# A post-norm attention and low-rank-expert layer: the FFN taken tile by tile, its narrow products joined to the wide ones, and the prior gathered first

## The chip, the cores and the metric

The kernel runs on one core of one Trainium2 chip. The metric is the device time of one execution in microseconds (us). A core has five engines that run side by side, each working through its own list of instructions in order: TensorE (PE: matrix products into PSUM banks), VectorE (DVE), ScalarE (ACT), GpSimd (POOL) and SyncE (SP, which only issues transfers here). An engine that reaches an instruction whose input is not ready stands still, and everything behind that instruction in its list stands with it. A PSUM bank that is to be written again must first have been read out.

## The reference

Two batches of 512 tokens, 512 features, all in 32-bit floats. The layer is two steps, each followed by a layer norm:

```
x = layernorm(x + attention(x))      # 32 query heads, 8 key/value heads of 128, causal, rotary
x = layernorm(x + ffn(x))

ffn(x):  y     = x @ W_base.T + b_base
         z_e   = x @ lora_A[e].T                     # 4 active experts of 16, rank 8
         alpha = softmax(log(prior + 1e-12) + router logits)     # over the 4 active ones
         y    += sum over e of alpha_e * 2 * (z_e @ lora_B[e].T)
```

The indices of the active experts are an input (`active`), so the rows of `lora_A`, `router_W`, `router_b`, `domain_prior` and `lora_B` have to be gathered at run time.

## The kernel before

The 1024 tokens are eight tiles of 128 (four per batch). Attention is 16 units (a key/value head of one batch) of four query tiles, so 64 parts; each part has four score blocks of 128 rows. The main loop is a software pipeline written out by hand: `slot(T)` issues one score block, and beside it pieces of work of other parts at fixed distances: projections for later units (L333, L346, and the query projection by Strassen products, L420), the softmax of the blocks before (maximum L487, exponential L494, reciprocal L498, normalise L502), the transposes of the probabilities (L510, L512), their way through DRAM (store, then `pT` load L528, both issued by SP), the product with the values (L535, `weigh`, into the one bank `pc` of the pool `ps_ctx`, copied out by ACT at L541), and the output projection (L420 for most parts, `wo_mm` L606 and `wo_out` L612 for the last eight). `put(slot, f)` hangs further work onto a slot. Nothing reorders this: the program is under a manual schedule, and every engine's list is the order in which the lines are written.

*The gathers.* POOL issues the loads of `active` early (L209 to L212: `act_e`, four of `act_er`, `act_p`). `gather_experts` runs in slot -8: eleven small integer operations on DVE turn the indices into row numbers, and POOL issues eight indirect gathers: A, router weights, router bias, prior, and four of B. In slots -4 to -2, `prior_weights` uses two of them: DVE adds a small number (L295), ACT takes the logarithm (L297), DVE adds the bias and spreads the row (L300, L304), and TensorE multiplies by the identity (`pl`, L307) so that all 128 partitions hold it. In slots 12 to 16 `lora_weights` transposes the gathered rows into `arT` (32 columns of A and 4 of the router) and `bmT` (B, with `b_base` as a 33rd row).

*The FFN.* `wbT` holds the transposed W_base. The class `Ffn` handles a group of tiles: `f0` is two pairs (batch 0), `fa` a pair, `fb` and `fc` one tile each (batch 1, whose last four parts are attended in the order 2, 3, 0, 1). For a tile x1T, the normed and transposed tokens, TensorE does:

- `route` (L665): four matmuls with the 36 columns of `arT`, giving `zl` (z and router logits), in a bank of its own;
- `base` (L712): four matmuls with the 512 columns of `wbT` into `py`;
- `low_rank` (L706): a transpose of `zs` (z times alpha), which DVE then copies (L707) to `zT`;
- `finish` (L716): one matmul of `zT` and `bmT` added into `py`; DVE adds x (L719) and takes the statistics for the second norm.

Between `route` and `low_rank` stand the softmax over the four experts (`logits` and `alphas`: DVE, ACT, DVE). The last tile `fc` does its W_base product in two halves (`half`, L727 to L729) whose banks DVE reads without an add. Each 32-bit matmul is two records in the trace.

A norm (`Norm`) is statistics on DVE, a square root on ACT (L631) and a reciprocal and a scaling on DVE (L635). Square root and exponential are different tables of ACT, so a change between them is an ACT_TABLE_LOAD. Stores of finished tiles are issued by SP, behind whatever stands before them in SP's list.

*Order.* With A = 245 as the slot in which the last Strassen output projection starts and E = 256 as the end of the score blocks: the first pair of `f0` does `route` at A+5, `base` at A+6 to A+9, the transposes at A+8, `finish` at A+10 and its stores at A+11. The second pair does `route` at A+13, its first tile's `base` at A+14 and A+15, and the rest in the tail, a list of calls behind the last slot. In that tail `base` of one tile stands between `route` and `low_rank` of another throughout:

```
    fa.low_rank()
    for c in range(KC):
        fa.base(1, c, *SC)
    fb.low_rank()
    fc.route(0)
```

Of the kernel before, what the change touches and what calls it, by code (L numbers as in the profile page):

```python
# [29 lines left out]
def postln_layer_kernel(  # L30
# [85 lines left out]
    bqkT = const.tile([P, H + G], F32, name="bqkT")  # L116
    arT = const.tile([P, KC, EAR + EA], F32, name="arT")
# [52 lines left out]
    nc.vector.memset(maskw, 0.0)  # L170
# [50 lines left out]
    def gather_experts():  # L221
# [25 lines left out]
        def gather(dst, src, idx):  # L247
            nc.gpsimd.indirect_dma_start(
                out=dst, out_offset=None, in_=src,
                in_offset=bass.IndirectOffsetOnAxis(ap=idx, axis=0),  # L250
            )

        gather(a_act, lora_A.rearrange("e r n -> (e r) n"), idx_a)
        gather(r_act, router_W, full_e)
        gather(rb_act, router_b.rearrange("(e o) -> e o", o=1), full_e)
        gather(pr_act, domain_prior.rearrange("(e o) -> e o", o=1), full_e)
        for a in range(EA):
            gather(b_act[:, a, :], lora_B.rearrange("e (p j) r -> (e p) (j r)", j=BJ), idx_b[:, a : a + 1])
# [379 lines left out]
    class Ffn:  # L638


        def __init__(self, name, tiles, pool, small_bank):
            self.name, self.pool, self.n = name, pool, len(tiles)
            self.small_bank = small_bank
            self.where = tiles
            self.tiles = [x_sb[:, t, :] for t in tiles]
            self.norm1 = Norm(pool, self.n, f"a{name}")
            self.norm2 = Norm(pool, self.n, f"f{name}")
            self.xT, self.py, self.y = {}, {}, {}

        def own(self, shape, name):  # L650
            return self.pool.tile(shape, F32, name=f"{name}_{self.name}")

        def centre(self, i):
            self.norm1.apply(i, self.tiles[i])

        def transpose(self, i, pool, tag):
            self.xT[i] = self.pool.tile([P, KC, P], F32, name=f"x1T_{self.where[i]}")
            transpose_token_tile(self.xT[i], self.tiles[i], pool, tag, nc.scalar.copy)

        def route(self, i):  # L660

            if i == 0:
                self.zl = self.small_bank[0].tile([P, self.n, EAR + EA], F32, tag=self.small_bank[1], name="zl")
            for c in range(KC):
                nc.tensor.matmul(  # L665
                    self.zl[:, i, :], lhsT=self.xT[i][:, c, :], rhs=arT[:, c, :],
                    start=(c == 0), stop=(c == KC - 1))

        def logits(self):
            n = self.n  # L670
            self.lg = self.own([P, n, EA], "lg")
            lp_all = lp_bc.unsqueeze(1).to_broadcast([P, n, EA])
            nc.vector.tensor_tensor(self.lg, self.zl[:, :, EAR:], lp_all, ALU.add)
            nmx = self.own([P, n], "nmx")
            nc.vector.tensor_reduce(nmx, self.lg, AX.X, ALU.max, negate=True)
            nc.vector.tensor_tensor(
                self.lg, self.lg, nmx.unsqueeze(2).to_broadcast([P, n, EA]), ALU.add)

        def alphas(self):

            n = self.n
            al = self.own([P, n, EA], "al")
            nc.scalar.activation(al, self.lg, AF.Exp)
            sm = self.own([P, n], "sm")
            nc.vector.tensor_reduce(sm, al, AX.X, ALU.add)
            nc.vector.reciprocal(sm, sm)
            nc.vector.tensor_scalar(sm, sm, SCALING, None, ALU.mult)
            nc.vector.tensor_tensor(al, al, sm.unsqueeze(2).to_broadcast([P, n, EA]), ALU.mult)
            self.zs = self.own([P, n, EA, RK], "zs")
            for i in range(n):  # L690
                nc.vector.tensor_tensor(
                    self.zs[:, i],
                    self.zl[:, i, :EAR].rearrange("p (a r) -> p a r", r=RK),
                    al[:, i, :].unsqueeze(2).to_broadcast([P, EA, RK]),
                    ALU.mult,
                )

        def ones(self):

            self.zT = self.own([EAR + 1, self.n, P], "zT")  # L700
            nc.gpsimd.memset(self.zT[EAR:, :, :], 1.0)

        def low_rank(self):
            tz = self.small_bank[0].tile([EAR, self.n, P], F32, tag=self.small_bank[1], name="tz")
            for i in range(self.n):
                nc.tensor.transpose(tz[:, i, :], self.zs[:, i].rearrange("p a r -> p (a r)"), ident)  # L706
            nc.vector.tensor_copy(self.zT[:EAR], tz)  # L707

        def base(self, i, c, pool, tag):
            if c == 0:  # L710
                self.py[i] = pool.tile([P, O], F32, tag=tag, name="py")
            nc.tensor.matmul(  # L712
                self.py[i], lhsT=self.xT[i][:, c, :], rhs=wbT[:, c, :], start=(c == 0), stop=False)

        def finish(self, i):
            nc.tensor.matmul(self.py[i], lhsT=self.zT[:, i, :], rhs=bmT, start=False, stop=True)  # L716
            t = self.where[i]
            self.y[i] = self.pool.tile([P, O], F32, name=f"y_{t}")
            nc.vector.tensor_tensor(self.y[i], self.py[i], self.tiles[i], ALU.add)  # L719
            self.norm2.stats(i, self.y[i])  # L720

        def half(self, i, n, pool, tag):

            cols = ts(n, O // 2)
            py = self.py[i, n] = pool.tile([P, O // 2], F32, tag=tag, name="ph")
            for c in range(KC):
                nc.tensor.matmul(py, lhsT=self.xT[i][:, c, :], rhs=wbT[:, c, cols], start=(c == 0), stop=False)  # L727
            nc.tensor.matmul(py, lhsT=ident, rhs=self.tiles[i][:, cols], start=False, stop=False)
            nc.tensor.matmul(py, lhsT=self.zT[:, i, :], rhs=bmT[:, cols], start=False, stop=True)  # L729

        def store(self, i):
            self.norm2.apply(i, self.y[i])
            nc.sync.dma_start(out=outf[ts(self.where[i], P), :], in_=self.y[i])

        def store_halves(self, i):
            t = self.where[i]
            y = self.pool.tile([P, O], F32, name=f"y_{t}")
            for n, queue in enumerate((nc.sync, nc.scalar)):
                cols = ts(n, O // 2)
                self.norm2.apply(i, y[:, cols], self.py[i, n])  # L740
                queue.dma_start(out=outf[ts(t, P), cols], in_=y[:, cols])
# [168 lines left out]
    for part in range(3):  # L910
        k_rope(0, part)

# [25 lines left out]
    wbT = ffn_pool.tile([P, KC, O], F32, name="wbT")  # L938
# [4 lines left out]
    K_BANK, WX, WY = (ps_k, "k"), (ps_wo, "wx"), (ps_wo, "wy")  # L943
    QX, QY, SC = (ps_q, "qx"), (ps_q, "qy"), (ps_sc, "sc")
    f0 = [Ffn(f"0{n}", [2 * n, 2 * n + 1], ffn_pool, K_BANK) for n in range(2)]
    fa = Ffn("1a", [TPB + i for i in order[:2]], ffn_pool, K_BANK)
    fb = Ffn("1b", [TPB + order[2]], ffn_pool, WX)
    fc = Ffn("1c", [TPB + order[3]], ffn_pool, WY)
    for f in (*f0, fa, fb, fc):
        f.ones()  # L950
    E = T_END
    A = LAST + LAG_WO
    for c in range(OC):
        put(T_PROJ + (0, 1, 4, 5)[c], lambda c=c: nc.sync.dma_start(out=wb_sb[:, c, :], in_=W_base[ts(c, P), :]))
        put(T_PROJ + (4, 5, 8, 9)[c], lambda c=c: transpose_token_tile(wbT[:, :, ts(c, P)], wb_sb[:, c, :], ps_k, "k", nc.scalar.copy))
    put(A + 1, lambda: [f.norm1.root(0, 2) for f in f0])
    for n, f in enumerate(f0):
        for k in range(2):
            put(A + (-7, -6, 0, 0)[2 * n + k], lambda f=f, k=k: f.norm1.stats(k, f.tiles[k]))
            put(A + 1 + n, lambda f=f, k=k: f.centre(k))  # L960
            put(A + 3 + n, lambda f=f, k=k: f.transpose(k, *(QX, QY)[k]))

    for n, f in enumerate(f0):
        at = A + 5 + n * 8
        for k in range(2):
            put(at, lambda f=f, k=k: f.route(k))
        put(at, f.logits)
        put(at + 1, f.alphas)
        for k in range(2 - n):
            for c in range(KC):  # L970
                put(at + 1 + 2 * k + c // 2, lambda f=f, k=k, c=c: f.base(k, c, *(QX, QY)[k]))
        put(at + 3, f.low_rank)
    for k in range(2):
# [11 lines left out]
    for k in range(2):  # L985
        fa.centre(k)
# [6 lines left out]
    for c in range(KC):  # L993
        fz.base(1, c, *QY)
# [100 lines left out]
```

## Time and profile before

| | us |
|---|---|
| three runs | 845.39, 845.54, 847.07 (median 845.54) |
| the profiled execution | 845.97 |
| its span, first to last instruction | 844.2 |
| TensorE busy in it | 830.7 |
| VectorE busy | 595.3 |
| ScalarE busy | 348.2 |
| GpSimd busy | 276.6 |
| mean granted TensorE clock | 0.996 |

The profile page names an engine, a line of the kernel (L716), an operation and its tiles as output<-inputs, with buffer numbers left out. "x8" is the number of records. In the chain of work that ended last, each instruction is followed back to what released it, and the shares of the span are given by engine. A line of waits reads: the waiting engine, its tile and line, what released it, then microseconds in all, how often, and the longest. A line of the table by windows gives the stretch, its length, then for PE, PEld (TensorE's loading of weights, which overlaps its matmuls), DVE, ACT and POOL in turn the microseconds busy with the count of instructions in brackets, and last the granted TensorE clock (1.00 is full speed), the busy share of the transfers, and GB/s. A timeline line is the start, the duration, the engine, and in square brackets how long the engine had been idle and what released it.

### The profile page before, as it was taken

Reading aid. Unit: us, or ns where it says so; the run is one execution under the profiler, and the core shown is the slowest. Engines: PE = TensorE matmul, PEld = TensorE weight load, DVE = VectorE, ACT = ScalarE, POOL = GpSimd, SP = SyncE. Lnnn points to the kernel's source line nnn. Section 1 sums busy time; section 2 is a strip of 40 time slices with the busy share of each in tenths; the row PEclk is TensorE's granted clock in tenths of the full one; section 3 lists DMA queues with packets and bytes.
Section 4 is the critical chain, followed back from the end, with each engine's and each line's share of the span. In section 5 each row is a group of like instructions: output and inputs, shape, how many; then the busy total and the mean of one; then the engine's idle time right before and its main releaser. Section 6 shows DMA issues by size and latency. Waiting matters only on the chain.

```text
span 844.2 us, 10656 instructions
## 1 busy us (share of the span) xinstructions
PE 830.7 (98%) x3179; PEld 578.1 (68%) x3179; DVE 595.3 (71%) x1955; ACT 348.2 (41%) x988; POOL 276.6 (33%) x307
## 2 busy tenths in 40 slices
PE   8989999999999999999999999999999999999997
PEld 5557677777777777777777777777777776645453
DVE  3458977778767876687767876687767868953545
ACT  1125454544435343434435443434435344662321
POOL 5375333422342334222342334334333523300000
PEclk9999999999999999999999999999999999999999
DMA  9016536445553546354553547275544536574302
GB/s 288 34 28 193 142 108 175 138 125 175 133 151 103 175 121 191 83 151 148 142 145 101 175 128 195 72 201 148 148 127 125 175 92 195 166 244 114 87 1 75
DMA packets 84971, 116.47 MB, mean 138 GB/s; under 512 B 6581, under 2 KB 64797, under 8 KB 82866
## 3 DMA queue, kind: packets, MB, share of 16 engines
q1 hardware_dynamic: 84258, 115.50, 48.0%
q0 software_dynamic: 448, 0.14, 0.3%
q8 instruction: 25, 0.41, 0.2%
q14 instruction: 32, 0.26, 0.1%
q10 hardware_dynamic: 208, 0.15, 0.1%
HBM read 71.73 MB, written 44.04 MB: 137 GB/s over the span
## 4 chain that ended last, share of the span: by engine, by line
PE 92%; DVE 4%; DMA 1%; POOL 1%; ACT 1%; issue 1%; SPq 0%; DVEq 0%; POOLq 0%
PE pc L535 16%; PE sc L479 13%; PE qx L420 11%; PE wx L420 11%; PE pp L346 9%; PE qy L420 8%; PE wy L420 8%; PE pv L333 7%; PE py L712 3%; PE po L606 3%; PE tp L265 1%; PE py L716 1%; PE zl L665 1%; DMA x_sb<-_attn_hidden_states_dram 1%; PE ph L727 0%
## 5 line engine op out<-in xcount | busy, mean ns | idle before, releaser
L494 ACT ACTIVATE p<-sc,nmax 128x288 f32<-128x288 f32 (+15 forms) x256 | 124.2, 485 | 266.0 <-DVE nmax L487 209.3
L487 DVE CUSTOM_DVE_ANT_0 sc<-sc,maskw 128x288 f32<-128x288 f32 (+15 forms) x256 | 114.2, 446 | 153.6 <-PE sc L479 150.9
L535 PE MATMUL pc<-pT,v 128*128 128x512 f32 x320 | 165.5, 600 | 0.0
L479 PE MATMUL sc<-kT,qT 128*128 128x160 f32 (+15 forms) x512 | 161.9, 398 | 1.3 <-ACT p L494 1.2
L502 ACT ACTIVATE p<-p,den 128x288 f32<-128x288 f32 (+15 forms) x256 | 133.5, 522 | 1.2 <-DVE den L498 1.0
L367 POOL TENSOR_TENSOR qT<-q,t 128x512 f32<-128x512 f32 x56 | 71.0, 1267 | 189.1 <-DVE q L366 189.1
L479 PEld LDWEIGHTS sc<-kT,qT 128*128 128x128 f32 x512 | 96.8, 190 | 31.0 <-issue 14.6
L407 POOL TENSOR_TENSOR cs<-ctxT 128x256 f32<-128x256 f32 x28 | 26.8, 956 | 195.6 <-PE wy L420 109.2
L541 ACT COPY ctxT<-pc 128x512 f32<-128x512 f32 x64 | 37.5, 586 | 119.3 <-PE pc L535 119.2
L510 DVE STREAM_TRANSPOSE zt<-p 128x128 f32<-128x128 f32 (+2 forms) x192 | 81.6, 425 | 0.0
L535 PEld LDWEIGHTS pc<-pT,v 128*128 128x128 f32 x320 | 56.9, 190 | 20.0 <-issue 6.4
L346 PE MATMUL pp<-xT,wk 128*128 128x512 f32 x128 | 65.0, 593 | 0.5 <-ACT xT L266 0.5
L333 PE MATMUL pv<-wv,xT 128*128 128x256 f32 x256 | 64.8, 385 | 0.0
L333 PEld LDWEIGHTS pv<-wv,xT 128*128 128x128 f32 x256 | 49.4, 194 | 14.1 <-issue 7.2
L420 PE MATMUL wx<-wo,ctxT 128*128 128x256 f32 x224 | 57.7, 380 | 0.4 <-DVE den L498 0.4
L420 PE MATMUL qx<-xs,wq 128*128 128x256 f32 x224 | 58.0, 381 | 0.0
L512 DVE STREAM_TRANSPOSE zt<-p 128x32 f32<-128x32 f32 (+3 forms) x256 | 57.4, 224 | 0.1
L420 PEld LDWEIGHTS qx<-xs,wq 128*128 128x128 f32 x224 | 41.4, 190 | 22.3 <-issue 16.0
L420 PEld LDWEIGHTS wx<-wo,ctxT 128*128 128x128 f32 x224 | 42.4, 190 | 13.5 <-issue 7.6
L494 ACT ACTIVATION_READ_ACCUMULATOR p<-sc,nmax 128x1 f32 x256 | 49.8, 195 | 0.0
L592 DVE TENSOR_TENSOR x_sb<-wx,x_sb 128x256 f32<-128x256 f32 x112 | 47.0, 419 | 0.0
L359 DVE SCALAR_TENSOR_TENSOR t<-q,bqkT,rope_sb 64x512 f32<-64x512 f32 x56 | 43.0, 768 | 1.3
(228 smaller groups left out, 1340.2 us busy)
## 6 DMA issues: line engine op xcount, KB each, us to landing
db<-zt SPq DMA_DIRECT2D x64, 256.0 KB, 4.0
pT<-db SPq DMA_DIRECT2D x16, 1024.0 KB, 4.8
db<-zt SPq DMA_DIRECT2D x64, 192.0 KB, 3.3
pT<-db SPq DMA_DIRECT2D x16, 768.0 KB, 4.4
wq<-in_L_attn_Wq_dram SPq DMA_DIRECT2D x20, 512.0 KB, 4.7
wo<-in_L_attn_Wo_dram SPq DMA_DIRECT2D x10, 1024.0 KB, 7.4
db<-zt SPq DMA_DIRECT2D x64, 128.0 KB, 2.4
pT<-db SPq DMA_DIRECT2D x16, 512.0 KB, 4.1
```

The source lines that it names most:

```text
L333: nc.tensor.matmul(psq["v", gg, t], lhsT=xT[:, c, ts(t, P)], rhs=wvs[gg][0][:, c, :], start=(c == 0), stop=(c == KC - 1))
L346: nc.tensor.matmul(psq[key], lhsT=wt[:, c, cols], rhs=xT[:, c, ts(b, S)], start=(c == 0), stop=(c == KC - 1))
L367: nc.gpsimd.tensor_tensor(dst, t1[:].rearrange("p (n s) -> p n s", s=BLK), t2[:].rearrange("p (n s) -> p n s", s=BLK), ALU.add)
L420: nc.tensor.matmul(ps, lhsT=wt[:, c, :], rhs=xt[:, c, :], start=start and c == 0, stop=c == CH - 1, skip_group_check=True)
L479: nc.tensor.matmul(sc[s][:, :w], lhsT=qT[u][:, i * QB + n].rearrange("p r s -> p (r s)"), rhs=kT[u][:].rearrange("p n s -> p (n s)")[:, :w ...
L487: nc.vector.tensor_tensor_reduce(sc[s][:, :w], sc[s][:, :w], maskw[:, S - w :], -SCALE, -MASKED, ALU.add, ALU.min, nmax[s])
L494: nc.scalar.activation(ptile[s][:, :w], sc[s][:, :w], AF.Exp, bias=nmax[s], scale=-1.0, accum_out=rden[s])
L502: nc.scalar.activation(ptile[s][:, :w], ptile[s][:, :w], AF.Copy, scale=rden[s])
L510: nc.vector.transpose(z[:, :, last - i : last, n, :].rearrange("p q j s -> p j q s"), ptile[s][:, : i * P])
L512: nc.vector.transpose(z[:, : n + 1, last, n, :], ptile[s][:, i * P : w])
L535: nc.tensor.matmul(psc[p], lhsT=v_sb[g // VG, b * TPB + j][:, ts(g % VG, D)], rhs=pT[p][:, :, ts(j, P)], start=(j == 0), stop=(j == i))
L592: nc.vector.tensor_tensor(into, pw[k, bank], into, ALU.add)
```

## The change

The diff has these parts:

1. **Columns joined.** `wbT` becomes two halves of 276 columns: 256 of W_base, then 16 of A, and in the second half 4 more of the router. POOL copies the columns of `arT` in. `base` writes two banks (`new_banks`) with 272 and 276 columns, and z and the router logits come out behind the products. `route` remains for the last tile alone, in eight matmuls of 16 and 20 columns.
2. **Tile by tile.** `Ffn` is for one tile, and `tiles()` makes several that share their norms. `logits` no longer subtracts the maximum; ACT's exponential takes it as its bias and sums in the same instruction, and the factor 2 goes into the multiplication. `low_rank` and `finish` are called one directly behind the other; `finish` is two matmuls of 256 columns, and two adds.
3. **Order.** Four tiles of `f0` start at A+5, A+10, A+12 and, in the tail, the fourth, `fz`. Second norm and stores of the first three are together at A+15. The tail is written anew.
4. **Gathers.** The index operations and the gathers of the prior and the router bias, the prior first, go into `expert_rows`, called right behind the first key rope; the other six gathers stay in slot -8.
5. The memset of `maskw` is two halves; the row of ones in `zT` is set per tile.

```diff
     bqkT = const.tile([P, H + G], F32, name="bqkT")
+
+    OH, ARH = O // 2, EAR // 2
+    WX_COLS = OH + ARH + EA
...
-    nc.vector.memset(maskw, 0.0)
+    for n in range(2):
+        nc.vector.memset(maskw[:, ts(n, S // 2)], 0.0)
...
-    def gather_experts():
+    idx = {}
+
+    def expert_rows():
...
-        gather(a_act, lora_A.rearrange("e r n -> (e r) n"), idx_a)
-        gather(r_act, router_W, full_e)
+        idx.update(a=idx_a, b=idx_b, e=full_e)
+        gather(pr_act, domain_prior.rearrange("(e o) -> e o", o=1), full_e)
         gather(rb_act, router_b.rearrange("(e o) -> e o", o=1), full_e)
-        gather(pr_act, domain_prior.rearrange("(e o) -> e o", o=1), full_e)
...
+    def gather_experts():
+        gather(a_act, lora_A.rearrange("e r n -> (e r) n"), idx["a"])
+        gather(r_act, router_W, idx["e"])
         for a in range(EA):
...
+        def new_banks(self):
+            self.py = [pool.tile([P, WX_COLS], F32, tag=tag, name="py") for pool, tag in self.banks]
+            self.z = [py[:, OH:] for py in self.py]
+
+        def base(self, c):
+            if c == 0:
+                self.new_banks()
+            for n in range(2):
+                w = OH + (ARH, WX_COLS - OH)[n]
                 nc.tensor.matmul(
...
+                    self.py[n][:, :w], lhsT=self.xT[:, c, :], rhs=wbT[:, c, n, :w], start=(c == 0), stop=(c == KC - 1),
+                    skip_group_check=True)
+
+        def route(self, pool, tag):
+
+            zl = pool.tile([P, 2, WX_COLS - OH], F32, tag=tag, name="zl")
+            for n in range(2):
+                w = (ARH, WX_COLS - OH)[n]
+                for c in range(KC):
+                    nc.tensor.matmul(
+                        zl[:, n, :w], lhsT=self.xT[:, c, :], rhs=wbT[:, c, n, OH : OH + w],
+                        start=(c == 0), stop=(c == KC - 1))
+            self.z = [zl[:, n, :] for n in range(2)]
...
-            nc.scalar.activation(al, self.lg, AF.Exp)
-            sm = self.own([P, n], "sm")
-            nc.vector.tensor_reduce(sm, al, AX.X, ALU.add)
+            al = self.own([P, EA], "al")
+            sm = self.own([P, 1], "sm")
+            nc.scalar.activation(al, self.lg, AF.Exp, bias=self.nmx, accum_out=sm)
             nc.vector.reciprocal(sm, sm)
-            nc.vector.tensor_scalar(sm, sm, SCALING, None, ALU.mult)
-            nc.vector.tensor_tensor(al, al, sm.unsqueeze(2).to_broadcast([P, n, EA]), ALU.mult)
+            nc.vector.tensor_scalar(al, al, sm, SCALING, ALU.mult, ALU.mult)
...
         def low_rank(self):
-            tz = self.small_bank[0].tile([EAR, self.n, P], F32, tag=self.small_bank[1], name="tz")
-            for i in range(self.n):
-                nc.tensor.transpose(tz[:, i, :], self.zs[:, i].rearrange("p a r -> p (a r)"), ident)
+            tz = ps_k.tile([EAR, P], F32, tag="k", name="tz")
+            nc.tensor.transpose(tz, self.zs.rearrange("p a r -> p (a r)"), ident)
             nc.vector.tensor_copy(self.zT[:EAR], tz)
...
+        def finish(self):
+            for n in range(2):
+                nc.tensor.matmul(
+                    self.py[n][:, :OH], lhsT=self.zT, rhs=bmT[:, ts(n, OH)], start=False, stop=True,
+                    skip_group_check=True)
+            for n in range(2):
+                nc.vector.tensor_tensor(self.y[:, ts(n, OH)], self.py[n][:, :OH], self.x[:, ts(n, OH)], ALU.add)
+            self.norm2.stats(self.i, self.y)
...
     for part in range(3):
         k_rope(0, part)
+    expert_rows()
...
+    nc.gpsimd.tensor_copy(wbT[:, :, 0, OH : OH + ARH], arT[:, :, :ARH])
+    nc.gpsimd.tensor_copy(wbT[:, :, 1, OH:], arT[:, :, ARH:])
...
+    f0 = tiles(range(TPB), ((QX, QY), (QX, QY), (SC, SC), (QX, QY)), "0")
+    fa = tiles([TPB + i for i in order[:2]], ((SC, SC), (WX, WY)), "1a")
+    (fb,) = tiles([TPB + order[2]], ((QX, QY),), "1b")
+    (fc,) = tiles([TPB + order[3]], ((SC, SC),), "1c")
...
+    put(A + 1, lambda: f0[0].norm1.root(0, TPB))
+    for k, f in enumerate(f0):
...
+        at = A + (5, 10, 12, 100)[k]
+        for c in range(KC):
+            put(at + c // 2, lambda f=f, c=c: f.base(c))
+        put(at + 2, lambda f=f: (f.logits(), f.alphas()))
+        put(at + 3, lambda f=f: (f.low_rank(), f.finish()))
+    put(A + 15, lambda: (f0[0].norm2.root(0, 3), [f.store() for f in f0[:3]]))
...
     for r in range(R):
         wo_mm(NP - 2, r)
     wo_out(NP - 2)
     for j in range(2):
         weigh(NP - 1, j)
     context_out(NP - 1)
...
+    base(fz)
...
+    fz.logits()
+    fz.alphas()
+    base(fa[0])
+    fb.transpose(*CTX)
+    fz.low_rank()
+    fz.finish()
+    fa[0].logits()
+    fa[0].alphas()
+    base(fa[1])
+    fc.transpose(*CTX)
+    fa[0].low_rank()
+    fa[0].finish()
+    fc.route(*CTX)
+    fc.logits()
+    fc.alphas()
+    fa[1].logits()
+    fa[1].alphas()
+    base(fb)
+    fc.low_rank()
+    fa[1].low_rank()
+    fa[1].finish()
+    fb.logits()
+    fb.alphas()
+    fz.norm2.root(3, 4)
+    fz.store()
+    fc.half(0)
+    fa[0].norm2.root(0, 2)
+    for f in fa:
+        f.store()
+    fb.low_rank()
+    fb.finish()
+    fc.half(1)
+    fb.norm2.root(0, 1)
+    fb.store()
...
```

## The prediction, made before the changed kernel was run

> **What bounds the kernel now.** I read the page first, then who waited for whom, then the windows around the two stretches in which the granted clock is below 1, then the timeline of the end.
>
> ```profile
> PE 830.7 (98%) x3179; PEld 578.1 (68%) x3179; DVE 595.3 (71%) x1955; ACT 348.2 (41%) x988; POOL 276.6 (33%) x307
> PE 92%; DVE 4%; DMA 1%; POOL 1%; ACT 1%; issue 1%; SPq 0%; DVEq 0%; POOLq 0%
> ```
>
> TensorE is busy 98% of the span and is 92% of the chain that ended last: matmul time saved on it is saved at the end, and an idle microsecond of it is lost, unless something else becomes late.
>
> ```profile
> PE pl L307 <- DVE lp_rep L304: 3.2, 1, 3.2
> PE sc L479 <- ACT p L494: 1.2, 1, 1.2
> ```
>
> These are the two largest TensorE waits after the first loads. The first is the prior: L307 multiplies a tile that needs the gather of the prior, the fourth of eight gathers.
>
> ```profile
> 44.00:45.00 1.00, 0.51 (x3) 0.49 (x4) 0.96 (x3) 0.59 (x1) 0.69 (x2) 1.00 0.01 2
> 45.00:46.00 1.00, 1.00 (x2) 0.44 (x2) 0.17 (x2) 0.00 (x0) 0.69 (x2) 0.60 0.09 16
> 46.00:47.00 1.00, 1.00 (x3) 0.59 (x2) 0.37 (x1) 0.00 (x0) 0.97 (x2) 0.50 0.09 16
> 47.00:48.00 1.00, 1.00 (x3) 0.76 (x3) 0.39 (x1) 0.00 (x0) 1.00 (x1) 0.50 0.50 34
> 48.00:49.00 1.00, 1.00 (x5) 0.83 (x4) 0.00 (x0) 0.00 (x0) 0.92 (x3) 0.69 0.67 193
> 826.00:828.00 2.00, 2.00 (x4) 0.63 (x3) 1.86 (x6) 1.16 (x2) 0.00 (x0) 0.71 0.00 0
> 828.00:830.00 2.00, 2.00 (x4) 0.75 (x3) 1.89 (x6) 0.29 (x1) 0.00 (x0) 0.50 0.00 0
> 830.00:832.00 2.00, 2.00 (x6) 0.73 (x4) 0.71 (x2) 0.00 (x0) 0.00 (x0) 0.93 0.44 163
> ```
>
> Behind the wait the clock (third figure from the right) is 0.5 for about 3.4 us: 0.40 + 0.50 + 0.50 + 0.31 = 1.71 us lost. It drops again at 826 to 831: 0.58 + 1.00 + 0.14 = 1.72 us lost, with no TensorE wait in front.
>
> ```profile
> 823.65 0.27 PE L706 MATMUL tz<-ident,zs_1b 128*32 128x128 f32 x1
> 823.75 0.98 PE L665 MATMUL zl<-arT,x1T 128*128 128x36 f32 x8
> 824.66 1.98 PE L716 MATMUL py<-bmT,zT_1a 33*128 33x512 f32 x4
> 835.42 0.70 PE L729 MATMUL ph<-bmT,zT_1c 33*128 33x256 f32 x2
> 823.96 0.28 DVE L707 COPY zT_1b<-tz 32x128 f32<-32x128 f32 x1 [2.11 <-PE tz L706]
> 825.58 1.28 ACT L631 ACT_TABLE_LOAD   x1
> 792.93 0.58 ACT L541 COPY ctxT<-pc 128x512 f32<-128x512 f32 x1 [1.99 <-PE pc L535]
> 794.96 0.52 SPq L528 DMA_DIRECT2D pT<-db  x1
> ```
>
> To be seen: after every transpose of `zs` (L706) other matmuls stand before L716, which needs the copied result. TensorE never waits there.
>
> **The sum's base.** The profiled execution took 845.97 us: its span of 844.2 and 1.77 around it. It lies 0.43 above the median of the runs, 845.54. The difference found below is added to the median.
>
> **Head: the prior first.** Removed: 3.16 us of idle (timeline: TensorE would have reached L307 at 44.49 - 3.16 = 41.33) and the 1.71 us behind it. With the prior landed early, the step that adds PRIOR_EPS on DVE can follow the L359 that runs at 38.86 for 0.76, so at 39.62; from its start (42.91) to L307 (44.49) took 1.58, so L307 is ready at 41.20, 0.13 before TensorE comes. Gain 4.87 us.
>
> What is moved forward: eleven small DVE operations, which took from 35.70 to 37.22, 1.52 us, now behind the first rope (it ends at 14.79), and two gathers on POOL, about 1.2 us each (starts 39.71, 40.90, 42.09). The DVE operations read loads that POOL issues from 5.75 to 9.13; the first took 6.0 us to land, the last (`act_p`, issued 8.55) is not shown. At 6.0 it lands at 14.6, at 7.5 at 16.0. So the next L359 (15.95 before) starts between 16.3 and 17.0. It is covered: DVE then idled 1.22 us before its L359 at 19.45; and TensorE needs the bank of that head only at 20.7, where before it was free at 18.2. Price 0; without that cover (`act_p` after 17.5) each later microsecond is one of TensorE. POOL's two gathers run 16.1 to 18.6 where its next add came at 18.31; it then idled 2.26 us, so 0. The six other gathers begin earlier. The halved mask memset frees the three warm-up matmuls some 0.2 us sooner, in front of a wait for the x tiles: 0.
>
> **Matmul time of the FFN.** Sixteen records of L665 are two tiles' eight matmuls in 1.71 us, 0.214 each. Removed: 8 tiles x 4 x 0.214 = 6.85. Added: the last tile's own routing, now 8 matmuls, 1.71; for seven tiles the columns: 548 in place of 512 at 0.858 per 512 (L712), 0.060 x 4 x 7 = 1.69; L716 takes 0.955 per 512 (1.91 for two), two halves about 0.52 each by L728/L729, +0.09 x 7 = 0.6. Sum **-2.85 us**. POOL's two small copies into `wbT` and eight memsets come where POOL is otherwise done (it has no work after 740): 0. SP's W_base loads are not moved.
>
> **New waits of TensorE.** The instruction order of the changed kernel shows five.
>
> (a) `low_rank` and `finish` are now one step: transpose, DVE copy, bias-and-B matmul with nothing between, at seven places (four tiles of the first sequence, two of the second, and one transpose that must wait for the copy of the bank's former content). Price from the rows: transpose 823.65, next matmul at 823.75, copy done at 824.24, handover 0.05 (44.44 to 44.49 at L307), first weights 0.1: 0.6. Lower end 0.5, upper 1.2, if DVE is in a softmax group. I take the near row: 7 x 0.6 = 4.2. Queued behind each: all of TensorE.
>
> (b) The first L535 of part 62 now follows the last of part 61 directly, where L712 stood between. It needs the one context bank: 792.73 to the end of the copy at 793.51, 0.8; the tile's Exp stands before that copy on ACT and can add 0.6. I take 1.2.
>
> (c) On SP the three stores of the first tiles now stand before the last `pT` load, and wait for the norm. From the third tile's last L716: half add 0.6, statistics 0.9, root and reciprocal 0.5, three scalings 1.5, store issue 0.4, landing 3.8 (issued 794.96, landed 798.77): 7.8 us. TensorE has 8 po matmuls meanwhile, 8 x 0.86 = 6.9. Wait 1.0; ends 0 and 2.
>
> (d) Near the end the tile `fb`: on DVE its logits stand behind the last `fa` tile's add and statistics, and its copy of zT behind the root and the three scalings of earlier tiles. From that L716: 0.6 + 0.9, logits and maximum 0.4, Exp 0.35, table load 1.28, root 0.3, reciprocal 0.2, scalings 0.5 + 0.2 + 1.0, copy 0.2: 5.9. TensorE has a half of 2.98 and the transpose: 3.1. Wait **2.8**, ends 1.5 and 4.2. Here the Trainium skill speaks against the row: "ScalarE: Activation LUTs", What ACT_TABLE_LOAD costs, gives a switch about 2.66 us, a drain included. The trace has 1.28, and the root starts 0.02 us after (825.58, then 826.88). By the page the wait would be 4.2; I go by the row.
>
> (e) The transpose of `fz` is 0.3 early for its `zs`.
>
> Sum of waits 4.2 + 1.2 + 1.0 + 2.8 + 0.3 = **9.5**.
>
> **The clock at the end.** The skill's "TensorE: Matmul & The Clock Gate", Part 1, names idle windows of some 3.4 us as the cause of half clock, and Part 4 says that transposes do not count as busy in the same way. By the first alone the drop at 826 could not be: TensorE was busy. What stands before it is a transpose, narrow L665 and L716 with 33 rows, so I read a window by its full matmuls. By the idle rule the changed end has one window in danger, (d), in place of none: +1.7. By my reading there was one before and there is again about one, as (d) joins 33-row matmuls to 2.8 us of idle: 0. I take 0.
>
> **Sum:** -4.87 - 2.85 + 9.5 = +1.8; with 0.2 for the last tile's statistics now split between two late halves: +2.0. 845.54 + 2.0 = **847.5 us**.
>
> **Rivals.** *Cheap hand-backs* (the other side): the price of (a) is what decides. At 0.32 instead of 0.6, at seven places, the two kernels are equal; at 0.1 each, and (d) shorter by 0.6, it is 843.4. For it: the DVE is 30% busy at 760 to 780. Against: the rows of copy and handover alone are 0.5. *More half-clock windows*: (a), (d) and the last tile's eight narrow matmuls give one or two more: 849.2 to 850.9. For it: the drop at 826. Against: the drop did not come at 811 to 815, where 1.7 us of L665 stood together. *The head does not pay*: L307 still waits because its margin is 0.13, or `act_p` is late and stalls the ropes: the 4.87 shrinks to 0 to 2, 850.4 to 852.4. Against: the gather has 20 us of lead.
>
> **How the numbers follow.** Forecast 0.50 (its own range 845.9 to 849.2), cheap hand-backs 0.22, more half-clock 0.20, head 0.08. A measurement tells about 0.2%, 1.7 us: the bounds are 843.85 and 847.23. In that order, faster: 0.01 + 0.14 + 0 + 0 = 0.15; same: 0.17 + 0.08 + 0 + 0 = 0.25; slower: 0.32 + 0 + 0.20 + 0.08 = 0.60. The range, 843.3 to 851.0, leaves out half of the second case's lower part and the ends of the last two, under 0.2.
>
> **What would show it.** Head right: no wait at the prior's matmul and clock 1.00 from 40 to 50. Waits right: TensorE waits of 0.5 to 0.7 on DVE `zT` at six places, 1 us on `pT`, near 3 on the last-but-one `zT`. Wrong: these waits under 0.3, a wait at the prior, or clock 0.5 in two stretches after 750.

## The result, and the profile after

Six runs took 849.01 to 851.03 us, median 850.38, against 845.50 for the kernel before (six runs, 845.37 to 847.91): ratio 1.0048, 95% interval 1.0033 to 1.0063. The change makes the kernel slower by 4.9 us by the medians, and by 4.1 us (2.8 to 5.3) by the ratio; the forecast was 847.5, slower by 2.0. The profiled execution took 850.84 us, its span 849.1, so the two profiles differ by 4.9 as well and can be compared piece by piece.

The page of the changed kernel, busy time and chain by engine:

```profile
PE 831.3 (98%) x3201; PEld 587.0 (69%) x3201; DVE 599.9 (71%) x1970; ACT 347.2 (41%) x996; POOL 277.3 (33%) x312
PE 91%; DVE 5%; ACT 1%; DMA 1%; issue 1%; POOL 1%; DVEq 0%; SPq 0%; POOLq 0%
```

TensorE is busy as long as before (831.3 against 830.7), although the FFN has less matmul time and the stretch of half clock in the head is gone. Much of the loss stands in TensorE's waits:

```profile
PE py L726 <- DVE zT L722: 5.4, 7, 2.6
PE pc L544 <- DMA pT<-db: 1.4, 2, 1.2
...
PE pc L544 <- ACT ctxT L550: 0.9, 1, 0.9
...
PE tz L721 <- DVE zs L712: 0.4, 1, 0.4
PE tz L721 <- DVE zT L722: 0.4, 1, 0.4
```

The wait at the prior is gone, and the five kinds of wait that the instruction order had shown are there. In the timeline of TensorE, the head first (the prior's matmul L316 and the first score block L488), then one hand-back, part 62, part 63 and the tile `fb`:

```profile
40.94 0.38 PE L316 MATMUL pl<-ident,lp_rep 4*128 4x4 f32 x2
45.66 0.30 PE L488 MATMUL sc<-kT,qT 128*128 128x32 f32 x2
...
765.26 0.27 PE L721 MATMUL tz<-ident,zs 128*32 128x128 f32 x1
765.99 1.10 PE L726 MATMUL py<-bmT,zT 33*128 33x256 f32 x4 [0.46 <-DVE zT L722]
...
785.77 1.02 PE L544 MATMUL pc<-pT,v 128*128 128x512 f32 x2
787.67 1.12 PE L544 MATMUL pc<-pT,v 128*128 128x512 f32 x2 [0.87 <-ACT ctxT L550]
...
798.75 1.98 PE L544 MATMUL pc<-pT,v 128*128 128x512 f32 x4 [1.22 <-DMA pT<-db]
...
833.69 0.28 PE L721 MATMUL tz<-ident,zs 128*32 128x128 f32 x1
836.59 2.00 PE L726 MATMUL py<-bmT,zT 33*128 33x256 f32 x4 [2.61 <-DVE zT L722]
```

The same first score block in the kernel before:

```profile
50.90 0.30 PE L479 MATMUL sc<-kT,qT 128*128 128x32 f32 x2
```

So the head leads by 50.90 - 45.66 = 5.24 us, and after 760 the kernel loses all of that and 4.9 us more. Part of that is in the clock. The windows of the changed kernel at its end (stretch, length, then busy time and count of PE, PEld, DVE, ACT and POOL, the granted clock, the share of transfers, GB/s):

```profile
819.58:823.00 3.42, 3.01 (x21) 2.65 (x22) 1.99 (x5) 0.46 (x1) 0.00 (x0) 1.00 0.02 5
823.00:826.41 3.41, 3.41 (x8) 2.48 (x8) 1.84 (x12) 0.78 (x4) 0.00 (x0) 0.51 0.00 0
833.24:836.66 3.42, 0.81 (x4) 0.29 (x4) 2.30 (x9) 1.39 (x3) 0.00 (x0) 1.00 0.16 61
836.66:840.07 3.41, 3.41 (x8) 2.31 (x9) 1.73 (x4) 0.04 (x1) 0.00 (x0) 0.50 0.44 169
840.07:843.48 3.41, 3.41 (x9) 2.31 (x8) 1.05 (x3) 0.25 (x1) 0.00 (x0) 0.50 0.20 77
```

Three stretches of 3.41 us at half clock, with TensorE busy in all of them: 5.1 us lost. The end of the kernel before had one, 1.7 us lost, behind a window in which TensorE was never idle:

```profile
823.43:826.85 3.42, 3.42 (x15) 1.92 (x14) 1.88 (x10) 1.47 (x2) 0.00 (x0) 1.00 0.00 0
826.85:830.26 3.41, 3.41 (x5) 1.35 (x5) 3.24 (x9) 0.61 (x3) 0.00 (x0) 0.50 0.00 0
```

The edges of one profile lie on one grid: in the changed kernel, from 823.00 to 836.66 is four times 3.415; in the kernel before, from the drop in the head (45.20) to the one at the end (826.85) is 229 times 3.413. In these profiles, then, the granted clock changes at edges that lie whole windows of about 3.413 us apart.

### The profile page after: what moved, and what is told of

It reads as the page before. It is cut to its first block, busy times and chain, and to the rows that moved or that the text cites. A ratio compares the mean times of both kernels' runs of the same rounds, so it can differ in the third digit from the quotient of the medians.

```text
span 849.1 us, 10726 instructions
## 1 busy us (share of the span) xinstructions
PE 831.3 (98%) x3201; PEld 587.0 (69%) x3201; DVE 599.9 (71%) x1970; ACT 347.2 (41%) x996; POOL 277.3 (33%) x312
## 4 chain that ended last, share of the span: by engine, by line
PE 91%; DVE 5%; ACT 1%; DMA 1%; issue 1%; POOL 1%; DVEq 0%; SPq 0%; POOLq 0%
PE pc L544 16%; PE sc L488 13%; PE qx L429 11%; PE wx L429 11%; PE pp L355 9%; PE qy L429 8%; PE wy L429 8%; PE pv L342 7%; PE py L681 3%; PE po L615 2%; PE tp L274 1%; DMA pT<-db 1%; PE py L726 1%; DVE st L636 1%; DVE wt L568 0%
## 5 line engine op out<-in xcount | busy, mean ns | idle before, releaser
L488 PE MATMUL sc<-kT,qT 128*128 128x160 f32 (+15 forms) x512 | 161.9, 398 | 1.1 <-ACT p L503 1.1
L488 PEld LDWEIGHTS sc<-kT,qT 128*128 128x128 f32 x512 | 96.8, 190 | 30.5 <-issue 14.3
```

The costliest lines, as they stand in the source:

```text
L488: nc.tensor.matmul(sc[s][:, :w], lhsT=qT[u][:, i * QB + n].rearrange("p r s -> p (r s)"), rhs=kT[u][:].rearrange("p n s -> p (n s)")[:, :w ...
```

## The experiments

Ten kernels were run, each beside the kernel before on the same chip; those chips spread the single times more than the first one did, so ratios are compared. The first four rows were run together, then the next four, then the last two. Each run also has a mean granted clock. Span times (1 - mean clock), averaged over the runs of a kernel, is called clock loss below. The clock is given to 0.001, so only means of several runs are used. A part of it lies behind the last matmul, where it costs nothing: in the profiles 0 to 1.7 us where the end behind the last matmul is 5.1 to 5.2 us long, and 1.8 to 2.7 us where it is longer (e3, e7, e8 and e9). So clock losses are best compared between kernels whose ends are equally long.

| kernel | median us (runs) | before beside it | ratio, 95% interval | clock loss |
|---|---|---|---|---|
| e1_head_only | 841.36 (9) | 845.08 | 0.9947 (0.9927 to 0.9967) | 2.6 |
| e2_ffn_only | 854.65 (6) | 845.08 | 1.0115 (1.0093 to 1.0137) | 8.0 |
| e3_fb_first | 846.35 (12) | 845.08 | 1.0006 (0.9987 to 1.0024) | 3.7 |
| e5_after_rows128 | 846.45 (12) | 845.08 | 1.0018 (1.0001 to 1.0034) | 2.6 |
| a2_after_again | 849.57 (12) | 844.94 | 1.0056 (1.0039 to 1.0074) | 6.3 |
| e4_head_rows128 | 836.02 (6) | 844.94 | 0.9885 (0.9861 to 0.9909) | 0.8 |
| e7_all_covered | 841.82 (12) | 844.94 | 0.9958 (0.9941 to 0.9975) | 3.8 |
| e8_all_rows128 | 838.70 (6) | 844.94 | 0.9917 (0.9893 to 0.9941) | 2.2 |
| e10_before_rows128 | 843.00 (12) | 846.18 | 0.9961 (0.9944 to 0.9978) | 3.2 |
| e9_end_on_dve | 837.94 (6) | 846.18 | 0.9905 (0.9874 to 0.9936) | 1.8 |

The kernel before has a clock loss of 4.0 to 4.8 in these runs, and the changed one 6.5 in its first six.

Three theories were to be told apart. The first: the loss is TensorE's new waits, plus half clock that follows windows in which TensorE does little work, be it idle, or busy with matmuls of few rows. The rival: only idle time lowers the clock, and the waits are the whole cause. The third: the FFN's new form is dearer by itself, and the waits only cover another bound.

### The head alone, and the FFN alone

The kernel before with the head's edit (the moved gathers and the halved memset of `maskw` go with the line shown):

```diff
     for part in range(3):
         k_rope(0, part)
+    expert_rows()
```

> The kernel before with the head of the change alone: index operations and the gathers of prior and router bias behind the first key rope, prior first, and the mask memset in halves. If the 5.55 us by which the changed kernel leads at every exponential of the main loop come from the head alone and lie on the path, this takes 845.5 - 5.5 = 840.0 us, no wait at the prior's matmul, clock 1.00 from 40 to 50. If the lead is absorbed later (a main loop bound elsewhere), 843 to 845.5.

Ratio 0.9947, 4.5 us faster (2.8 to 6.2): 5.5 is inside. In the profile there is no wait at the prior, and the exponentials of the main loop start 5.5 to 5.7 us earlier than in the profile of before, up to the last parts. It was not absorbed. But the profiled run took 842.03 and not 840.0, since it has two windows of half clock before the last matmul in place of one, with TensorE at work throughout (same columns as above):

```profile
809.20:812.60 3.40, 3.40 (x6) 1.41 (x5) 2.82 (x13) 0.87 (x2) 0.00 (x0) 0.54 0.00 0
...
822.90:826.30 3.40, 3.40 (x5) 1.39 (x5) 3.23 (x9) 0.62 (x3) 0.00 (x0) 0.53 0.00 0
```

The FFN in this kernel is that of before, only 5.7 us earlier. How many windows it gets depends on where they fall.

The changed kernel with the head undone (`gather_experts` as before):

```diff
     for part in range(3):
         k_rope(0, part)
-    expert_rows()
```

> The changed kernel with the head undone: eight gathers together at slot -8, the prior the fourth, mask memset in one piece; the FFN tile by tile as in the change. If head and FFN only add, 850.4 + 5.5 = 855.9 us. If the windows of the clock fall differently, since everything comes 5.5 us later, up to 1.7 less or more: 854.2 to 857.6. If the FFN part were worth nothing by itself, 845.5.

Ratio 1.0115, 9.7 us slower. Head and FFN add: -4.5 + 9.7 = +5.2, beside the +4.1 and +4.7 of the two measurements of the whole. So the FFN part alone loses twice what the whole shows. Its profile holds a surprise in the head. The prior's wait of 3.2 us is back, and yet the clock behind it is 1.00. The 1.71 us of half clock behind that wait, which the prediction counted as gained, are lost in one execution and not in another.

The grid shows a difference between the two. In e2_ffn_only it can be carried back from the drop at 824.34, by 229 steps of 3.413, to an edge at 42.69. First the window of the kernel before that holds the wait, then three windows of e2_ffn_only:

```profile
41.78:45.20 3.42, 0.70 (x3) 0.59 (x4) 2.18 (x7) 1.49 (x2) 2.50 (x4) 1.00 0.06 9
...
39.28:42.69 3.41, 1.48 (x4) 0.38 (x2) 0.33 (x2) 0.18 (x1) 2.62 (x3) 1.00 0.02 3
42.69:46.10 3.41, 2.19 (x9) 1.59 (x10) 2.49 (x7) 1.30 (x2) 2.67 (x3) 1.00 0.07 14
46.10:49.51 3.41, 3.41 (x13) 2.08 (x12) 1.73 (x6) 0.24 (x2) 3.32 (x4) 1.00 0.55 161
```

In the kernel before most of the wait fell into one window, which had TensorE busy for 0.70 us only. In e2_ffn_only an edge cut the wait in two, and no window had less than 1.48. This fits, and no run tests it by itself.

### The hand-back of fb ahead of norms and stores

```diff
+    fc.half(0)
+    fb.low_rank()
     fz.norm2.root(3, 4)
     fz.store()
-    fc.half(0)
     fa[0].norm2.root(0, 2)
     for f in fa:
         f.store()
-    fb.low_rank()
     fb.finish()
```

> The changed kernel with the transpose and copy of the tile fb ahead of the second norms' roots and scalings and the stores of fz and fa, so that DVE copies zT at once and table loads stand behind. TensorE's wait of 2.61 falls to about 0.2 (-2.4). If the two windows of half clock at 836.7 to 843.5 come from that idle time, they go too: -3.4 more, 844.6 us. If they come from the narrow and 33-row matmuls whatever the waits, 848.0. If the scalings moved behind make the end later instead, 849 to 850.

```profile
PE py L726 <- DVE zT L722: 3.1, 7, 0.5
```

The wait of 2.6 is now 0.4, and the windows behind it are gone from the profile, with the one at 823 (here 822) left. By ratio 1.0006 against 1.0056 and 1.0048, 3.5 to 4.2 us are won for 2.2 us of idle, and the clock loss falls from 6.3 to 3.7. A part of what was left is lost at the end, since the scalings now stand there: from the last matmul to the end it is 6.0 us, not 5.1. So wait and clock go together. The gain lies between the expectation's two sums, 2.4 us for the wait alone and 5.8 with two windows.

### 128 rows in place of 33

```diff
-            self.zT = ffn_pool.tile([EAR + 1, P], F32, name=f"zT_{t}")
-            nc.gpsimd.memset(self.zT[EAR:, :], 1.0)
+            self.zT = ffn_pool.tile([P, P], F32, name=f"zT_{t}")
+            nc.gpsimd.memset(self.zT, 0.0)
+            nc.gpsimd.memset(self.zT[EAR : EAR + 1, :], 1.0)
...
+    bmP = ffn_pool.tile([P, O], F32, name="bmP")
+    nc.gpsimd.memset(bmP, 0.0)
+    nc.gpsimd.tensor_copy(bmP[: EAR + 1, :], bmT)
```

with `bmP` for `bmT` in the matmuls. Every wait stays. In the changed kernel:

> The changed kernel with zT and B padded with zeros from 33 to 128 rows: the same number of matmuls of the same length, but with all rows at work. If a window counts by the work done in it, the window of half clock at 840.1, which follows one with 2.0 us of 33-row matmuls, goes: 850.4 - 1.7 = 848.7 us, with the drop at 823 staying (narrow columns) or going too (847.0). If only idle time counts, or the columns alone, 850.4.

Ratio 1.0018, and the unaltered kernel in the next runs:

> The changed kernel unaltered, beside its variants on one chip. 850.4 us and a mean clock of 0.992 to 0.993 as in its first runs, so that span times (1 - clock) is about 6.5 us. If the 4 us by which the 128-row variant was faster were a matter of the chip, this comes out at 846.5 here.

It is slow there too (1.0056), so padding is worth about 3.2 us of its 4.7 (2.5 of 4.1 by the first measurement), and clock loss falls from 6.3 to 2.6, with ends equally long (5.1 and 5.2 us). The new profile of the unaltered kernel again has three windows of half clock before the last matmul, 5.1 us in all, but shared otherwise:

```profile
821.28:824.70 3.42, 3.42 (x13) 2.97 (x13) 1.54 (x10) 0.39 (x2) 0.00 (x0) 0.50 0.00 0
824.70:828.11 3.41, 3.41 (x9) 2.55 (x8) 0.71 (x5) 0.39 (x2) 0.00 (x0) 0.50 0.00 0
...
838.35:841.76 3.41, 3.41 (x9) 2.52 (x8) 2.63 (x7) 0.29 (x1) 0.00 (x0) 0.50 0.20 78
```

Two begin during the last tile's `route`, and one stands behind the wait of `fb`. The same holds in e2_ffn_only; in the first profile it was one and two.

In the profile of the padded kernel the wait of `fb` is as long as ever (2.65 us). Its windows, on the grid carried back from the drop at 842.26:

```profile
818.37:821.78 3.41, 2.99 (x22) 2.88 (x23) 2.16 (x6) 0.41 (x1) 0.00 (x0) 1.00 0.01 2
821.78:825.19 3.41, 3.41 (x16) 2.73 (x15) 1.69 (x12) 0.78 (x4) 0.00 (x0) 1.00 0.00 0
825.19:828.61 3.42, 2.52 (x12) 1.86 (x11) 1.75 (x5) 0.00 (x0) 0.00 (x0) 1.00 0.00 0
828.61:832.02 3.41, 2.04 (x10) 1.29 (x8) 1.89 (x10) 2.15 (x5) 0.00 (x0) 1.00 0.00 0
832.02:835.43 3.41, 1.85 (x9) 1.64 (x10) 2.54 (x8) 0.00 (x0) 0.00 (x0) 1.00 0.60 231
835.43:838.84 3.41, 1.87 (x9) 1.32 (x7) 2.55 (x9) 0.59 (x2) 0.00 (x0) 1.00 0.20 77
```

There is no half clock up to the last matmul (it ends at 837.3). The first window compares well with that of the changed kernel at 819.58 to 823.00: busy for 2.99 and 3.01 us, the same matmuls and the same kind of wait, but without 33-row matmuls no drop follows. So the narrow columns of the last tile's `route` (16 and 20, at 819.7 to 821.4 here) did not do it alone. For the wait of `fb` this profile proves less. An edge cut the wait in two, and TensorE was busy for 2.04 and 1.85 us in the two windows, against 0.81 in the changed kernel; there the mean over the runs has to speak. Idle time is not free of blame: 2.6 of clock loss is more than the 0.8 of the next kernel, which has no such wait and an end as long.

The same edit on the kernel before with the new head, and on the kernel before alone:

> The kernel before with the head of the change and with zT and B padded with zeros to 128 rows, the FFN otherwise as before. The profiled run of the head alone had three windows of half clock in the last 40 us. If a window counts the work done in it, the 33-row matmuls are their cause, and span times (1 - clock) falls from 2.6 to about 1: 839.5 us. If only idle time or narrow columns count, the head alone's 841.4. If the extra rows cost time, more than 841.4.

> The kernel before, nothing changed but zT and B padded with zeros from 33 to 128 rows. If the 33-row matmuls cause the half clock of the tail, only the head's window is left: span times (1 - clock) falls from about 4 to 2.5 or less (1.7 of the head and 0.8 behind the last matmul), and the time from 845.0 to 842 or somewhat lower. If the padding helped only together with the new head, 845.

The first gives 0.9885, 9.7 us faster than before, and 5.2 faster than the head without it. More than was expected. Its end, ten microseconds at a time:

```profile
800.00:810.00 10.00, 10.00 (x46) 6.09 (x44) 3.29 (x12) 3.35 (x6) 0.00 (x0) 1.00 0.01 2
810.00:820.00 10.00, 10.00 (x42) 5.62 (x41) 6.62 (x28) 2.10 (x4) 0.00 (x0) 1.00 0.00 1
820.00:829.20 9.20, 9.20 (x35) 6.10 (x33) 7.53 (x19) 0.95 (x4) 0.00 (x0) 1.00 0.36 133
```

TensorE is never idle here and the clock is 1.00 throughout; the six runs lie within 0.75 us (835.52 to 836.27). Between the two profiles the last matmul ends 5.9 us earlier, and 3.4 of that are the two windows of half clock. What the expectation missed is that the rows are not free to leave out. Two tiles' matmuls with B, then the next product, in the head alone and in this kernel:

```profile
807.68 2.04 PE L722 MATMUL py<-bmT,zT 33*128 33x512 f32 x4
809.64 5.29 PE L718 MATMUL py<-wbT,x1T 128*128 128x512 f32 x8
```

```profile
806.76 1.88 PE L723 MATMUL py<-bmP,zT 128*128 128x512 f32 x4
808.48 3.60 PE L719 MATMUL py<-wbT,x1T 128*128 128x512 f32 x8
```

From start to start it is 1.96 us with 33 rows and 1.72 with 128: 0.12 a tile more for fewer rows. (The 5.29 behind the first is the half clock.)

The second, without the new head, gives 0.9961: 3.3 us, clock loss from 4.8 to 3.2. Its profile has no drop from 780 to the last matmul, and again none behind the prior's wait of 3.2 (the clock is 1.00 from 41 to 51). It has one at 76.7 to 80.1 instead, behind a wait of 1.57 us for a `pT` load. TensorE was busy for 1.83 us in the window ahead of that drop (73.29 to 76.70), and for 1.45 us in the first of the two windows that share the prior's wait (39.16 to 42.57), which no drop followed. So the busy time of a window does not decide alone, and where the limit lies these runs do not show.

### All waits covered

The changed kernel with a step of other matmuls between every `low_rank` and its `finish`, `f0[2]` a slot later, the three stores behind the last `pT` load, `fb` as above, and scalings on POOL but for the last tile:

```diff
-        put(at + 3, lambda f=f: (f.low_rank(), f.finish()))
-    put(A + 15, lambda: (f0[0].norm2.root(0, 3), [f.store() for f in f0[:3]]))
+        late = at + (k == 1)
+        put(late + 3, f.low_rank)
+        put(late + 4, f.finish)
...
-    fz.low_rank()
-    fz.finish()
     fa[0].logits()
     fa[0].alphas()
-    base(fa[1])
+    base(fa[1], (0, 1))
+    fz.low_rank()
+    base(fa[1], (2, 3))
+    fz.finish(False)
+    fa[0].low_rank()
+    fz.finish_out()
     fc.transpose(*CTX)
-    fa[0].low_rank()
     fa[0].finish()
...
```

> The changed kernel with the waits covered: a step of other matmuls between every transpose of zs and the matmul that needs its copy; the third tile of f0 a slot later, so that part 62's first matmul no longer follows part 61's last; the first three stores behind the last load of pT; fb's copy ahead of norms and stores; scalings of all but the last tile on POOL. Of 9.9 us of waits some 2 remain (f0's third transpose and fa's first copy come late by 1.3 and 0.5), and the end grows by 0.5: 850.4 - 7.4 = 843.0 us if as many windows of half clock stay, 839.6 if two go with the idle time. If the waits only hid a bound of DVE or ACT, 847 to 850.

Ratio 0.9958, 841.82: between the expectation's two sums. Against the changed kernel beside it, 7.8 us are gone by the medians, although the end behind the last matmul is now 7.8 us long in place of 5.1. Clock loss falls by 2.5. So the waits were the cost, not a cover over another bound. The profile has two windows of half clock left before the last matmul, from 817.7 to 824.5, and in the window ahead of them TensorE was busy for 3.39 of 3.42 us, with 33-row matmuls, transposes and narrow routing. With 128 rows:

> The same with zT and B padded to 128 rows. If work per window sets the clock, hardly a window of half clock is left before the last matmul: 836 to 838 us, mean clock 0.998 or more. If idle time alone sets it, as the kernel without padding.

In this profile there is no half clock before the last matmul, although TensorE stands still once in the last 20 us before it (0.6 us) and in e7_all_covered never. So idle time was not what made the two windows there. The clock loss over the runs falls from 3.8 to 2.2, and all that this profile has (2.7) lies behind the last matmul. The time is 838.70, 2.7 more than the head with 128 rows, though TensorE's last matmul ends earlier here (827.9 against 829.3). The end behind it is 8.1 us long in place of 5.1, and the chain that ends last runs through POOL. From the timeline of POOL in e8_all_rows128:

```profile
826.33 4.13 POOL L644 TENSOR_SCALAR y<-y,mv_f1a,rstd_f1a 128x512 f32<-128x512 f32 x2 [4.20 <-DVE rstd_f1a L641]
830.43 2.07 POOL L644 TENSOR_SCALAR y<-y,mv_f1b,rstd_f1b 128x512 f32<-128x512 f32 x1
```

A scaling that takes DVE 0.54 takes POOL 2.07, and SP's queue holds the last store behind it. Moving one of the three back:

```diff
     fb.norm2.root(0, 1)
-    fb.store(nc.gpsimd)
     fc.norm2.stats(0, *fc.py)
+    fb.store()
     fc.norm2.root(0, 1)
```

> The changed kernel with all waits covered and 128 rows, and with the scaling of the tile fb on DVE, behind the statistics of fc, instead of on POOL, where one takes 2.07 us against 0.54 and the last stores waited for it. The end behind the last matmul falls from 8.2 us to 5.5 to 6.2: 838.7 - 2.0 to 2.7 = 836.0 to 836.7 us, level with the head alone plus 128 rows (836.0). If joined columns are worth their 2.6 us of matmul time once the waits are gone, 834 to 835; if the end stays bound by POOL, 838.7.

837.94, ratio 0.9905 (0.9874 to 0.9936), not to be told from the 0.9917 before it, and short of the 836.0 to 836.7 expected: the two of `fa` remain on POOL, and the end is still 7.2 us long. Whether joined columns would win with a better end was not tried. The best kernel of the study is the one with the fewest edits: the new head, the old FFN, 128 rows, at 836.02 us.

## Why the prediction was right and wrong

Right: the sign, the range (843.3 to 851.0), and the steps in their places. Wrong: the size, by 2.9 us, and nearly all of it in one step. That the range held owes something to its width: 850.38 lies 0.6 below its upper end, and came by a branch that was given a chance of 0.20. The prediction's steps against the profile of the changed kernel:

| step | predicted us | measured us | from |
|---|---|---|---|
| head | -4.87 | -5.24, -5.55 later | first score block; exponentials from the 33rd on |
| matmul time of the FFN | -2.85 | -2.6 | lengths in the chain, below |
| (a) transpose, copy, matmul | 4.2 | 4.3 | six times 0.73 - 0.11, once 0.65 - 0.11 |
| (b) context bank | 1.2 | 1.04 | 787.67 - 785.77, less 0.86 |
| (c) stores ahead of `pT` | 1.0 | 1.2 to 1.5 | idle 1.22, and 0.27 more in the matmuls at the stop |
| (d) fb | 2.8 | 2.8 | 836.59 - 833.69, less 0.11 |
| (e) fz | 0.3 | 0.4 | waits |
| clock at the end | 0 | +3.4 | three windows, 5.1, in place of one, 1.72 |
| last tile's statistics | +0.2 | 0.0 | last matmul to end: 5.1 both times |
| sum | +2.0 | +5 | the profiled executions differ by 4.9 |

**The head.** The wait is gone, the margin held, and the eleven DVE operations cost nothing, as the step said. The last of them waited for `act_er` and `act_p` until 15.72, so the next rope began at 16.66, inside the 16.3 to 17.0 that the step gave. The 0.4 that came on top is the first 9 us: the warm-up matmuls start 0.27 earlier, and the x tile that TensorE had waited 0.32 for was there this time (by luck: in a2_after_again TensorE waits 0.3 for it). The part of this step that was weaker than it looked is the clock. Two other profiles have that same wait and clock 1.00, so 1.71 was a loss of the one profiled execution, not of every one.

**Matmul time.** A tile's product with joined columns takes 3.69 us in the chain against 3.43, near the 3.67 forecast; the last tile's own routing took 1.89 and not 1.71, as sixteen records of 16 to 20 columns are no shorter than those of 36.

**The waits.** All five kinds came, near the values taken. In (c) the listed times add up to 7.7, not 7.8, so that wait comes to 0.8 by its own terms and not 1.0. In (d) the row was right for the table load of ACT: the wait is 2.8, as with 1.28, where the 2.66 of the Trainium skill's "ScalarE: Activation LUTs", What ACT_TABLE_LOAD costs, would have made 4.2. The load took 1.28 again, 0.02 behind the exponential and 0.01 ahead of the root. That (c) comes from the stores is shown by e7_all_covered, where they stand behind the load: there the load of the last `pT` was issued at 785.91 and landed at about 789.6, and TensorE came to it at 796.09 without a stop.

**The clock.** This is the step that failed: "By my reading there was one before and there is again about one, as (d) joins 33-row matmuls to 2.8 us of idle: 0. I take 0." Its size was wrong: +3.4 us in the profile. The way of reading a window was right as far as it was tested. When the 33-row matmuls become 128-row ones, with TensorE's idle time unchanged, the half clock at the end goes away in the profiles of e5_after_rows128, e4_head_rows128, e10_before_rows128 and e8_all_rows128. Over the runs most of the clock loss goes too (6.3 to 2.6, and 2.6 to 0.8 with the new head), except in e10, where a third goes (4.8 to 3.2). The Trainium skill's "TensorE: Matmul & The Clock Gate", Part 1, which names idle windows, would have given +1.7; it has no place for the drop at 823, ahead of which TensorE was busy for 3.01 of 3.42 us, nor for the one of the kernel before (3.42 of 3.42).

What was mis-sized is the count of windows. There were two places, not one: the 33-row matmuls, the narrow routing and a 0.46 wait together in 819.6 to 823.0, and (d). And one of the two cost twice, (d) in this profile and the other place in a2_after_again and e2_ffn_only. In each case the first slow window itself began with 1.4 to 2.0 us of 33-row matmuls or narrow routing; where it held hardly anything but wide products, as at 823.0 here, no second one followed. That this work bought the second window is read from where the windows lie and was not tested apart. The rival "More half-clock windows", 849.2 to 850.9 at a chance of 0.20, is what happened: 850.38. The argument against it, that no drop had come at 811 to 815, was worth little. The head alone has a drop at 809 to 813 with the same FFN, so its absence in one profile said only where the windows lay in that execution.

**The other rivals.** Cheap hand-backs: no, 0.62 each and not 0.1. A head that does not pay: no.

## What to carry to other kernels

Where TensorE is the bound, look at the granted clock before you count matmul time. Here a bias-and-low-rank matmul of 33 rows was slower than one of 128 (0.98 against 0.86 a tile), and with it the clock loss over the runs was 1.6 to 3.7 us larger. Padding the contraction with zeros on an idle engine gave 3.3 us on the kernel before and 5.2 on the one with the new head; the joined columns of this change saved 2.6. A transpose whose copy feeds the next matmul wants another matmul between; seven such pairs put back to back cost 4.3 us. A single profile shows where the windows of half clock fell once: judge them by the mean clock of many runs, and price a clock gain of one window as uncertain.

## What was not expected of the hardware

A TensorE wait of 3.16 to 3.2 us in the head was followed by a half-clock window in one profile (before) and by none in two others (e2_ffn_only, e10_before_rows128). The windows are 3.41 us long, and the drops of one profile lie on a fixed grid. The Trainium skill's "TensorE: Matmul & The Clock Gate", Part 1, calls the window free-running, so that its start differs from one execution to the next. The profiles agree: the grid edge at the wait lies at 45.20 in the kernel before, where the wait ends at 44.49, and at 42.69 and 42.57 in the two others, where it ends at 43.91 and 43.79 and is cut in two. Three profiles are few, and no run moved the wait on purpose.

A 32-bit matmul with 33 rows took longer than one with 128, 1.96 us against 1.72 for two tiles' products. And POOL took 2.07 us for a 128x512 subtract-and-multiply that DVE did in 0.54.
